# The feed-forward of the last block, computed in two groups of two windows

## The chip, the cores and the metric

The kernel runs on one core of a Trainium2 chip. A core has a matrix engine (TensorE, "PE" in the profile), a vector engine (VectorE, "DVE"), a scalar engine (ScalarE, "ACT"), GpSimd ("POOL") and SyncE ("SP"), which here issues all transfers. "PEld" is the loading of weights into the matrix engine, which the profile lists apart from the matmuls ("PE"). The metric is the device time of one execution in microseconds, as the median of several executions. All data are float32.

## The reference

The input is a batch of 2 sequences of 4096 tokens with 256 channels. First a residual recurrence (time mixing, a scan along the sequence, a group norm, an output projection), then a residual stack of two transformer layers. One layer is

```python
h = shift_token(x)                         # half of the channels from the token before
q, k, v = split(h @ wqkv, 3)               # 8 heads of 64
q, k = rotary_xpos(l2norm(q) * qs, l2norm(k) * ks)
x = x + local_attention(q, k, v) @ wo      # windows of 128, each looks at itself and the one before
h = layernorm(shift_token(x)) * lg + lb
a, g = split(h @ w1 + b1, 2)               # 256 -> 2 x 682
x = x + (a * gelu(g)) @ w2 + b2            # 682 -> 256
```

The last four lines are the feed-forward that the change touches. Every token's feed-forward needs only that token's `x` after attention and half of the channels of the token before.

## The kernel before, in words

Tokens are tiled into windows of 128 (`P`), four windows (`NW`) make a block of 512 tokens (`T`), and there are `NK` = 32 blocks (2 sequences, 2 layers, 8 blocks). The main loop of `tile_block_kernel` runs over `n`, one step for each of the `NN` = 128 windows. A step does the attention of window `n`, prepares the projections of window `n + 1`, and finishes window `n - 1`: `values` (probabilities times values), `output` (the projection by `wo`, added to `x`), `shift` (three or four small transfers that write the shifted copy of `x` into the tile `h`, and in the second layer an addition on GpSimd), and one step later `normed` (layer norm of that window in `h`).

The feed-forward goes by whole blocks of 512 tokens, spread over the steps of the blocks that follow. `transpose_h` (line 1244) transposes the four windows of `h` by TensorE into two banks of PSUM, and ScalarE and VectorE write them, scaled and shifted by the layer norm's weights, into `hT` (channels on the partitions, tokens along the row). `hidden` (1260) multiplies 128 of the 1364 hidden units (106 in the one remainder) by all 512 tokens: two matmuls, one for each half of the 256 channels. In the profile each float32 matmul is two records, so one call of `hidden` is four records of PE. `gate` (1268) copies such a bank into `hm`, five times; `remainders` (1271) does the last 42 gate units and the last 42 value units together and lays odd windows on other partitions than even ones, in `ends` and `rem`. `gelus` (1283) is one piece of seven activations on ScalarE that nothing may be put between. `value` (1294) multiplies five further banks into `hm` and `rem` into `ends`. `down_ends` (1313) begins the second product of two windows with the remainders, on half of the matrix rows each so that two matmuls run beside each other; `down` (1325) adds the five full parts, adds the result to `x` and stores the window to `out` (second layer).

`fill` (1338) says in which step each part is recorded: gates in the step with `s == 1` of the block after, the rest of the gates, the remainders, the gelus and two values in `s == 2`, the other values in `s == 3`, the two down products two blocks later. After the last window the loop runs on for six steps (`range(NN + 6)`, line 1447), in which no attention is left and only the feed-forward of the last block is recorded.

What is recorded is not the order on the engines. `Plan.note` (238) only records operations, with the row `plan.at` as their priority. `Plan.order` (376) then builds the order of all five engines with a list scheduler: it keeps a model of when each engine and each of the 8 banks of PSUM comes free, and on each engine always takes, among what could start first by the model, the piece with the lowest row. Matmuls into one bank that follow each other are one piece. `value` sets `plan.early` in the last block, which lets the value products be computed before the gelus that they are multiplied with. Semaphores are set by the tile framework for exactly the tiles and parts of tiles that overlap. Line 524, which most rows of the profile name, is the place in `Plan.give` from which every recorded operation is issued; the tiles' names tell the operations apart (`hT,w` into a bank: `hidden`; `w,hm`: `down`; `w,ends`: `down_ends`; `wo,oT`: `output`; `mats,h`: `transpose_h`).

Of the kernel before, what the change touches and what calls it, by code (L numbers as in the profile page):

```python
# [11 lines left out]
ALU = mybir.AluOpType  # L12
# [3 lines left out]
P = 128  # L16
# [5 lines left out]
NM = 6  # L22
HR = HID - 5 * P
HS = 64 + HR
HW = 10 * P + HS
T = 512
NW = T // P
# [153 lines left out]
class Plan:  # L181
# [35 lines left out]
    def bank(self, shape):  # L217

        return self.view(Place(T, True), 0, shape)
# [308 lines left out]
def kernel(ctx: ExitStack, tc: tile.TileContext, a: dict, out: bass.AP):  # L528
# [6 lines left out]
    tile_of, bank, piece = plan.tile, plan.bank, plan.piece  # L535
    act, dve, either = nc.scalar.copy, nc.vector.tensor_copy, nc.either.copy
# [4 lines left out]
    ident, gmat = (mats[:, i, :] for i in range(2))  # L541
# [318 lines left out]
    def weights(l, which):  # L860
        if "qkv" in which:
            for j in range(3):
                cols = slice(j * INNER, (j + 1) * INNER)
                nc.sync.dma_start(out=wqkv[:, :, cols], in_=a["w_qkv"][l][:, :, cols])
        if "o" in which:
            nc.sync.dma_start(out=wo, in_=a["w_o"][l])
        if "1" in which:
            nc.sync.dma_start(out=w1, in_=a["w_1"][l])
        if "2" in which:
            nc.sync.dma_start(out=w2, in_=a["w_2"][l])  # L870
# [370 lines left out]
            nc.gpsimd.tensor_tensor(x[:, w, :], x[:, w, :], x1s[k][:, w, :], ALU.add)  # L1241
            plan.at(row)

    def transpose_h(k):
        l = blocks[k][0]
        h = hs.pop(k)
        hT = hTs[k] = tile_of([P, 2, T], "hT")
        for i in range(2):
            pt = bank([P, T])
            for w in range(NW):  # L1250
                nc.tensor.transpose(
                    pt[:, w * P : (w + 1) * P], h[:, w, i * P : (i + 1) * P], ident
                )
            g, bb = lnp[:, l, 0, i : i + 1], lnp[:, l, 1, i : i + 1]
            if i == 0:
                nc.scalar.activation(hT[:, i, :], pt, AF.Identity, bias=bb, scale=g)
            else:
                nc.vector.tensor_scalar(hT[:, i, :], pt, g, bb, ALU.mult, ALU.add)

    def hidden(k, c0, cols):  # L1260
        pm = bank([P, T])
        for i in range(2):
            nc.tensor.matmul(
                pm[:cols], w1[:, i, c0 : c0 + cols], hTs[k][:, i, :], start=(i == 0), stop=(i == 1)
            )
        return pm

    def gate(k, m):
        either(hm[:, m, :], hidden(k, m * P, P))

    def remainders(k):
        pm = hidden(k, G_LAST * P, HS)
        rems[k] = tile_of([P, NW // 2, P], "rem")
        for odd in range(2):
            rows = slice(64 * odd, 64 * odd + HR)
            nc.scalar.copy(ends[rows], of_half(pm[64:HS], odd))
            either(rems[k][rows], of_half(pm[:HR], odd))

    def of_half(t, odd):

        return t.rearrange("p (w two t) -> p w two t", two=2, t=P)[:, :, odd, :]

    def gelus(k):
        l = blocks[k][0]
        with piece():
            for m in range(NM - 1):
                g = hm[:, m, :]
                nc.scalar.activation(g, g, AF.Gelu, bias=b1[:, l, 1, m : m + 1])
            for odd in range(2):
                rows = slice(64 * odd, 64 * odd + HR)  # L1290
                g = ends[rows]
                nc.scalar.activation(g, g, AF.Gelu, bias=b1[rows, l, 1, NM - 1 : NM])

    def value(k, m):
        l = blocks[k][0]
        plan.early = k == NK - 1
        if m < NM - 1:
            src = hidden(k, G_LAST * P + HS + m * P, P)
            g = hm[:, m, :]
            nc.vector.scalar_tensor_tensor(g, src, b1[:, l, 0, m : m + 1], g, ALU.add, ALU.mult)  # L1300
        else:
            src = rems.pop(k)
            for odd in range(2):
                rows = slice(64 * odd, 64 * odd + HR)
                g = ends[rows]
                nc.vector.scalar_tensor_tensor(
                    g, src[rows], b1[rows, l, 0, m : m + 1], g, ALU.add, ALU.mult
                )
        plan.early = False

# [2 lines left out]
    def down_ends(n):  # L1313

        k, i = (n - NW) // NW - 1, n % NW
        if not 0 <= k < NK or i > 1:
            return
        for odd in range(2):
            rows = slice(64 * odd, 64 * odd + 64)
            pys[k, 2 * i + odd] = bank([P, D])  # L1320
            nc.tensor.matmul(
                pys[k, 2 * i + odd], ends[rows, i, :], w2[rows, NM - 1, :], start=True, stop=False
            )

    def down(k, w):
        py = pys.pop((k, w))
        for m in range(NM - 1):
            nc.tensor.matmul(
                py, hm[:, m, w * P : (w + 1) * P], w2[:, m, :], start=False, stop=(m == NM - 2)
            )  # L1330
        x = xs[k][:, w, :]
        nc.vector.tensor_tensor(x, x, py, ALU.add)
        l, b, c = blocks[k]
        o = c * T + w * P
        to = out[b, o : o + P, :] if l else xmd[b][c][:, w, :]
        nc.sync.dma_start(out=to, in_=x)

    def fill(n, i):

        s = n % NW  # L1340
        k = n // NW - 2
        if s < 2 and 0 <= k < NK and i == 0:
            down(k, 2 * s)
            down(k, 2 * s + 1)
        k = n // NW - 1
        if not 0 <= k < NK:
            return
        if s == 1:
            gate(k, i)
        elif s == 2:  # L1350
            if i == 0:
                gate(k, 4)
                remainders(k)
                gelus(k)
            elif i < 3:
                value(k, i - 1)
        elif s == 3 and i < 3:
            value(k, i + 2)
            if i == 2:
                value(k, 5)  # L1360

# [80 lines left out]
    norms(0)  # L1444
    cosines(0)
    rotated(0)
    for n in range(NN + 6):
        k, w = divmod(n, NW)
        here, ahead, behind = n < NN, n + 1 < NN, 0 < n <= NN
        plan.at(n)  # L1450
        if here:
            transpose_qk(n)
        for c in range(rec2.n):
            if NW + 1 + int(c * R_SLOTS / rec2.n) == n:
                plan.at(n + 0.5)
                if AHEAD <= c + 1 < rec2.n:
                    rec2.ahead(c + 1, rec2.mixed)
                elif INSIDE <= c + 1 < AHEAD:
                    rec2.back(c + 1)
                rec2.scans(c)  # L1460
                if c + 1 == rec2.n:
                    rec2.group_norm()
        plan.at(n)

        first, l = ahead and (n + 1) % (NB * NW) == 0, ((n + 1) // (NB * NW)) % L
        if w == 3 and k + 2 < NK:
            load(k + 2)
        if w == 0 and k + 1 < NK:
            mixed_out(k + 1)
        if 1 < n < NN + 2:  # L1470
            normed(hs[(n - 2) // NW][:, (n - 2) % NW, :])
        if ahead:
            table(n + 1)
            if first:
                weights(l, "qkv")
            project(n + 1, 0)
            rotate(n + 1, 0)
        if here:
            scores(n)
            differences(n)  # L1480
        else:
            with piece():
                if n == NN:
                    values(n - 1)
                down_ends(n)
        if behind:
            kept(n - 1)
        if here:
            softmax(n, 0)
            softmax(n, 1)  # L1490
        if ahead:
            project(n + 1, 1)
            square(n + 1)
            rotate(n + 1, 1)
        if behind:
            output(n - 1)
            shift(n - 1)
            if here and n % (NB * NW) == 0:
                weights(n // (NB * NW) % L, "o")
        if w == 1 and 0 < k <= NK:  # L1500
            transpose_h(k - 1)
        if w == 2 and k + 1 < NK:
            transpose_x(k + 1)
        if here:
            softmax(n, 2)
            softmax(n, 3)
        if ahead:
            norms(n + 1)
        fill(n, 0)
        if here:  # L1510
            transpose_p(n, 0)
        if ahead:
            project(n + 1, 2)
            cosines(n + 1)
        fill(n, 1)
        if here:
            transpose_p(n, 1)
        if ahead:
            rotated(n + 1)
        fill(n, 2)  # L1520
        fill(n, 3)
        if w < 2 and NW < n < NN and (n - NW - w) % (NB * NW) == 0:
            weights(n // (NB * NW) % L, "12"[w])
    with tc.manual_schedule():
        plan.give()

# [78 lines left out]
```

## Time and profile before

| | before |
|---|---|
| median of three runs | 2972.16 us (2969.49 to 2972.76) |
| the profiled execution's own time | 2970.99 us |
| its span, first to last instruction | 2969.2 us |
| mean granted TensorE clock | 0.998 |
| PE busy, PE weight loads busy | 2945.0 us (99%), 1913.7 us (64%) |
| DVE, ACT, POOL busy | 2250.9, 2018.8, 1449.3 us |
| PE's instructions | 15548 |

Times in the profile are microseconds from the first instruction. A row of the timeline is a start, a length, an engine, a line, an operation, its output and inputs, the shape, and a count when equal instructions follow each other; a number in brackets is idle time before it and what ended that. [...] the start of the next row, not the end of the one before, tells how long a group held the engine.

### The profile page before, as it was taken

How to read it: one execution, taken by the hardware profiler on the slowest of the kernel's cores; microseconds unless marked ns; L12 is line 12 of the kernel's file. 1: busy time of each engine (PE TensorE's matmuls, PEld its weight loads, DVE VectorE, ACT ScalarE, POOL GpSimd, SP SyncE). 2: the span in 40 equal slices, each digit the busy share in tenths (PEclk: the TensorE clock that was granted, in tenths of full speed). 3: DMA queues.
4: the chain of work that ended last, by engine and by line, in shares of the span. 5: the costliest groups of instructions: out<-in, count | busy, mean ns of one | idle time of the engine just before them, and what ended most of it. 6: DMA issues, size and time to landing. Idle time of an engine off the chain costs nothing.

```text
span 2969.2 us, 48964 instructions
## 1 busy us (share of the span) xinstructions
PE 2945.0 (99%) x15548; PEld 1913.7 (64%) x15548; DVE 2250.9 (76%) x5088; ACT 2018.8 (68%) x5359; POOL 1449.3 (49%) x1705
## 2 busy tenths in 40 slices
PE   9999999999999999999999999999999999999998
PEld 4476766666666666666666666666666666666665
DVE  7889999998866788786777677777676676767673
ACT  7887787778666777776666666666666666666663
POOL 2226654555554555445555444545454554555550
PEclk9999999999999999999999999999999999999999
DMA  2324322221121211111122221111112211111110
GB/s 85 114 78 133 115 69 87 75 82 53 60 65 54 83 48 53 56 59 55 52 77 79 74 68 48 61 58 61 55 44 70 70 57 49 58 55 54 47 40 27
DMA packets 185227, 195.09 MB, mean 66 GB/s; under 512 B 27812, under 2 KB 148484, under 8 KB 184456
## 3 DMA queue, kind: packets, MB, share of 16 engines
q1 hardware_dynamic: 184968, 191.96, 20.9%
q8 instruction: 123, 2.02, 0.3%
q14 instruction: 136, 1.11, 0.1%
HBM read 85.46 MB, written 39.85 MB: 42 GB/s over the span
## 4 chain that ended last, share of the span: by engine, by line
PE 92%; DVE 3%; ACT 3%; issue 1%; POOL 0%; DMA 0%; SPq 0%; POOLq 0%; ACTq 0%; DVEq 0%
PE bank L524 92%; ACT pr L524 1%; ACT L524 1%; DVE arena L524 1%; DVE bank L524 0%; ACT pr L520 0%; DVE sq L524 0%; DVE qk L524 0%; DVE h L524 0%; DVE nmx L524 0%; DVE hm L524 0%; DVE pB L524 0%; ACT arena L524 0%; ACT oT L524 0%; ACT hm L524 0%
## 5 line engine op out<-in xcount | busy, mean ns | idle before, releaser
L524 PE MATMUL bank<-wqkv,xT 128*128 128x512 f32 x1536 | 723.8, 596 | 0.5 <-ACT xT L524 0.5
L524 PE MATMUL bank<-hT,w 128*128 128x512 f32 (+1 forms) x1408 | 652.2, 595 | 0.0
L524 POOL TENSOR_TENSOR t<-qk,tab 128x256 f32<-128x256 f32 x512 | 383.6, 768 | 471.2 <-ACT qk L524 362.3
L524 ACT ACTIVATE pr<-bank,nmx 128x129 f32<-128x129 f32 (+1 forms) x1024 | 369.5, 379 | 147.8 <-DVE nmx L524 146.4
L524 PEld LDWEIGHTS bank<-hT,w 128*128 128x128 f32 (+1 forms) x1408 | 254.8, 189 | 260.9 <-issue 247.3
L524 PEld LDWEIGHTS bank<-wqkv,xT 128*128 128x128 f32 x1536 | 266.4, 191 | 210.9 <-issue 207.3
L524 POOL TENSOR_TENSOR rn<-rn,mhalf 128x16 f32<-128x16 f32 x128 | 391.7, 3060 | 8.8
L520 ACT ACTIVATE pr<-pr,sums 128x129 f32<-128x129 f32 (+1 forms) x948 | 334.1, 418 | 40.7 <-DVE pr L524 39.9
L524 DVE COPY_PREDICATED bank<-packs,bank 128x254 f32<-128x254 int32 x496 | 186.4, 420 | 229.8 <-PE bank L524 229.7
L524 PE MATMUL bank<-w,hm 128*128 128x256 f32 x1280 | 294.0, 381 | 0.0
L524 POOL TENSOR_TENSOR dv<-vr,vt 128x512 f32<-128x512 f32 x124 | 165.4, 1334 | 201.2 <-PE bank L524 188.1
L524 PEld LDWEIGHTS bank<-w,hm 128*128 128x128 f32 x1280 | 239.7, 190 | 35.0 <-issue 4.2
L524 ACT COPY qk<-bank 128x512 f32<-128x512 f32 x225 | 132.3, 588 | 170.5 <-PE bank L524 164.0
L524 PE MATMUL bank<-kT,qT 64*128 64x256 f32 (+1 forms) x2048 | 246.1, 380 | 0.4 <-ACT kT L524 0.4
L524 PE MATMUL bank<-wo,oT 128*128 128x256 f32 x1024 | 243.0, 380 | 1.4 <-ACT oT L524 1.3
L524 PEld LDWEIGHTS bank<-wo,oT 128*128 128x128 f32 x1024 | 193.4, 190 | 70.5 <-ACT oT L524 22.6
L524 PEld LDWEIGHTS bank<-kT,qT 64*128 64x128 f32 x2048 | 190.4, 187 | 68.8 <-issue 36.0
L524 DVE TENSOR_TENSOR pB<-bank,backs 128x512 f32<-128x512 f32 x248 | 170.0, 686 | 83.5 <-PE bank L524 56.7
L524 ACT ACTIVATION_READ_ACCUMULATOR pr<-bank,nmx 128x1 f32 x1024 | 221.8, 217 | 0.0
L524 ACT COPY hm<-bank 128x512 f32<-128x512 f32 x170 | 99.8, 587 | 174.1 <-PE bank L524 173.1
L524 PEld LDWEIGHTS bank<-mats,pr 128*128 128x128 f32 x1148 | 134.9, 135 | 115.7 <-issue 73.2
L524 PE MATMUL bank<-pT,vt 128*64 128x128 f32 x2048 | 203.3, 279 | 0.0
(159 smaller groups left out, 5625.3 us busy)
## 6 DMA issues: line engine op xcount, KB each, us to landing
vr<-vt SPq DMA_DIRECT2D x124, 224.0 KB
tab<-in_c_rot_dram SPq DMA_DIRECT2D x128, 128.0 KB
kT<-kT SPq DMA_DIRECT2D x64, 256.0 KB
z<-zd SPq DMA_DIRECT2D x16, 512.0 KB
x<-in_x_dram SPq DMA_DIRECT2D x16, 512.0 KB
x1d<-x SPq DMA_DIRECT2D x16, 512.0 KB
x<-x1d SPq DMA_DIRECT2D x16, 512.0 KB
h<-x SPq DMA_DIRECT2D x128, 64.0 KB
```

Of the source, the lines that this page charges most:

```text
L520: self.nc.scalar.activation(dst, src, AF.Copy, scale=scale)
L524: getattr(getattr(self.nc, o.eng), name)(*args, **kw)
```

## The change

In the loop, the last block's feed-forward is no longer recorded: the loop ends after `NN + 2` steps, `fill` stops before block `NK - 1`, and the transposes of that block are left out. Instead `last_block` is called after the loop. It takes the block's windows 0 and 1, and then 2 and 3, and records for each pair the whole feed-forward: transposes, five gates, the remainders, the gelus, six values and the two down products, at row `NN` for the first pair and `NN + 2` for the second (the down products are recorded in the row set there, too). For that `transpose_h`, `hidden`, `gate`, `remainders`, `gelus` and `value` take a stretch of tokens `ts`. All other blocks are computed as before, with 512 tokens in one piece.

```diff
@@ -1241,15 +1241,17 @@
             nc.gpsimd.tensor_tensor(x[:, w, :], x[:, w, :], x1s[k][:, w, :], ALU.add)
             plan.at(row)
 
-    def transpose_h(k):
+    def transpose_h(k, w0=0, w1=NW):
         l = blocks[k][0]
-        h = hs.pop(k)
-        hT = hTs[k] = tile_of([P, 2, T], "hT")
+        h = hs[k]
+        if w0 == 0:
+            hTs[k] = tile_of([P, 2, T], "hT")
+        hT = hTs[k][:, :, w0 * P : w1 * P]
         for i in range(2):
-            pt = bank([P, T])
-            for w in range(NW):
+            pt = bank([P, (w1 - w0) * P])
+            for w in range(w0, w1):
                 nc.tensor.transpose(
-                    pt[:, w * P : (w + 1) * P], h[:, w, i * P : (i + 1) * P], ident
+                    pt[:, (w - w0) * P : (w - w0 + 1) * P], h[:, w, i * P : (i + 1) * P], ident
                 )
             g, bb = lnp[:, l, 0, i : i + 1], lnp[:, l, 1, i : i + 1]
             if i == 0:
@@ -1257,54 +1259,57 @@
             else:
                 nc.vector.tensor_scalar(hT[:, i, :], pt, g, bb, ALU.mult, ALU.add)
 
-    def hidden(k, c0, cols):
-        pm = bank([P, T])
+    def hidden(k, c0, cols, ts):
+        pm = bank([P, ts.stop - ts.start])
         for i in range(2):
             nc.tensor.matmul(
-                pm[:cols], w1[:, i, c0 : c0 + cols], hTs[k][:, i, :], start=(i == 0), stop=(i == 1)
+                pm[:cols], w1[:, i, c0 : c0 + cols], hTs[k][:, i, ts], start=(i == 0), stop=(i == 1)
             )
         return pm
 
-    def gate(k, m):
-        either(hm[:, m, :], hidden(k, m * P, P))
-
-    def remainders(k):
-        pm = hidden(k, G_LAST * P, HS)
-        rems[k] = tile_of([P, NW // 2, P], "rem")
-        for odd in range(2):
-            rows = slice(64 * odd, 64 * odd + HR)
-            nc.scalar.copy(ends[rows], of_half(pm[64:HS], odd))
-            either(rems[k][rows], of_half(pm[:HR], odd))
+    ALL = slice(0, T)
+
+    def gate(k, m, ts=ALL):
+        either(hm[:, m, ts], hidden(k, m * P, P, ts))
+
+    def halves(ts):
+
+        pairs = slice(ts.start // (2 * P), ts.stop // (2 * P))
+        return [(odd, slice(64 * odd, 64 * odd + HR), pairs) for odd in range(2)]
+
+    def remainders(k, ts=ALL):
+        pm = hidden(k, G_LAST * P, HS, ts)
+        if ts.start == 0:
+            rems[k] = tile_of([P, NW // 2, P], "rem")
+        for odd, rows, pairs in halves(ts):
+            nc.scalar.copy(ends[rows, pairs], of_half(pm[64:HS], odd))
+            either(rems[k][rows, pairs], of_half(pm[:HR], odd))
 
     def of_half(t, odd):
-
         return t.rearrange("p (w two t) -> p w two t", two=2, t=P)[:, :, odd, :]
 
-    def gelus(k):
+    def gelus(k, ts=ALL):
         l = blocks[k][0]
         with piece():
             for m in range(NM - 1):
-                g = hm[:, m, :]
+                g = hm[:, m, ts]
                 nc.scalar.activation(g, g, AF.Gelu, bias=b1[:, l, 1, m : m + 1])
-            for odd in range(2):
-                rows = slice(64 * odd, 64 * odd + HR)
-                g = ends[rows]
+            for odd, rows, pairs in halves(ts):
+                g = ends[rows, pairs]
                 nc.scalar.activation(g, g, AF.Gelu, bias=b1[rows, l, 1, NM - 1 : NM])
 
-    def value(k, m):
+    def value(k, m, ts=ALL):
         l = blocks[k][0]
         plan.early = k == NK - 1
         if m < NM - 1:
-            src = hidden(k, G_LAST * P + HS + m * P, P)
-            g = hm[:, m, :]
+            src = hidden(k, G_LAST * P + HS + m * P, P, ts)
+            g = hm[:, m, ts]
             nc.vector.scalar_tensor_tensor(g, src, b1[:, l, 0, m : m + 1], g, ALU.add, ALU.mult)
         else:
-            src = rems.pop(k)
-            for odd in range(2):
-                rows = slice(64 * odd, 64 * odd + HR)
-                g = ends[rows]
+            for odd, rows, pairs in halves(ts):
+                g = ends[rows, pairs]
                 nc.vector.scalar_tensor_tensor(
-                    g, src[rows], b1[rows, l, 0, m : m + 1], g, ALU.add, ALU.mult
+                    g, rems[k][rows, pairs], b1[rows, l, 0, m : m + 1], g, ALU.add, ALU.mult
                 )
         plan.early = False
 
@@ -1343,7 +1348,7 @@
             down(k, 2 * s)
             down(k, 2 * s + 1)
         k = n // NW - 1
-        if not 0 <= k < NK:
+        if not 0 <= k < NK - 1:
             return
         if s == 1:
             gate(k, i)
@@ -1358,6 +1363,23 @@
             value(k, i + 2)
             if i == 2:
                 value(k, 5)
+
+    def last_block():
+
+        k = NK - 1
+        for w in (0, 2):
+            plan.at(NN + w)
+            ts = slice(w * P, (w + 2) * P)
+            transpose_h(k, w, w + 2)
+            for m in range(NM - 1):
+                gate(k, m, ts)
+            remainders(k, ts)
+            gelus(k, ts)
+            for m in range(NM):
+                value(k, m, ts)
+            down_ends(NN + NW + w // 2)
+            down(k, w)
+            down(k, w + 1)
 
 
 
@@ -1444,7 +1466,7 @@
     norms(0)
     cosines(0)
     rotated(0)
-    for n in range(NN + 6):
+    for n in range(NN + 2):
         k, w = divmod(n, NW)
         here, ahead, behind = n < NN, n + 1 < NN, 0 < n <= NN
         plan.at(n)
@@ -1497,7 +1519,7 @@
             shift(n - 1)
             if here and n % (NB * NW) == 0:
                 weights(n // (NB * NW) % L, "o")
-        if w == 1 and 0 < k <= NK:
+        if w == 1 and 0 < k < NK:
             transpose_h(k - 1)
         if w == 2 and k + 1 < NK:
             transpose_x(k + 1)
@@ -1521,6 +1543,7 @@
         fill(n, 3)
         if w < 2 and NW < n < NN and (n - NW - w) % (NB * NW) == 0:
             weights(n // (NB * NW) % L, "12"[w])
+    last_block()
     with tc.manual_schedule():
         plan.give()
 
```

## The prediction

> **What bounds the kernel now.** I read the page first, then the timeline of the matrix engine (PE) in the last 55 us, then the chain of waits there, then the other engines' timelines.
>
> ```profile
> PE 2945.0 (99%) x15548; PEld 1913.7 (64%) x15548; DVE 2250.9 (76%) x5088; ACT 2018.8 (68%) x5359; POOL 1449.3 (49%) x1705
> PE 92%; DVE 3%; ACT 3%; issue 1%; POOL 0%; DMA 0%; SPq 0%; POOLq 0%; ACTq 0%; DVEq 0%
> ```
>
> PE is busy for 99% and is 92% of the chain: only PE's idle time, or its own work, can move the end. The built orders are the same on all engines up to the last transposes of probabilities, so the change concerns what stands from 2915 us on:
>
> ```profile
> 2914.56 0.89 PE L524 MATMUL bank<-mats,pr 128*128 128x128 f32 x5
> 2915.38 0.70 PE L524 MATMUL bank<-w,ends 64*128 64x256 f32 x4
> ...
> 2922.43 0.70 PE L524 MATMUL bank<-w,ends 64*128 64x256 f32 x4
> 2923.06 2.43 PE L524 MATMUL bank<-w,hm 128*128 128x256 f32 x10
> 2925.32 1.89 PE L524 MATMUL bank<-wo,oT 128*128 128x256 f32 x8
> 2927.05 2.32 PE L524 MATMUL bank<-w,hm 128*128 128x256 f32 x10
> 2929.21 0.49 PE L524 MATMUL bank<-mats,h 128*128 128x128 f32 x3
> 2934.43 1.33 PE L524 MATMUL bank<-mats,h 128*128 128x128 f32 x5 [4.74 <-DVE h L524]
> 2935.78 20.10 PE L524 MATMUL bank<-hT,w 128*128 128x512 f32 x44
> 2955.81 0.70 PE L524 MATMUL bank<-w,ends 64*128 64x256 f32 x4
> 2956.44 4.58 PE L524 MATMUL bank<-w,hm 128*128 128x256 f32 x20
> 2960.95 0.70 PE L524 MATMUL bank<-w,ends 64*128 64x256 f32 x4
> 2961.59 4.58 PE L524 MATMUL bank<-w,hm 128*128 128x256 f32 x20
> ```
>
> After three transposes PE has nothing left until 2934.43: the last window's `h` is not ready. The chain shows what it waits for, behind the down product that SP's queue puts ahead of the last transfer:
>
> ```profile
> 2929.41 0.43 DVE x L524
> ...
> 2930.25 1.96 DMA h<-x
> ...
> 2933.96 0.42 DVE h L524
> ```
>
> And PE comes back at a lower clock. The windows of the trace (after the stretch and its length: busy time and count of PE, PEld, DVE, ACT, POOL, then the granted clock):
>
> ```profile
> 2930.00:2940.00 10.00, 5.55 (x13) 2.93 (x14) 1.83 (x4) 1.36 (x2) 1.49 (x3) 0.83 0.05 16
> 2940.00:2950.00 10.00, 10.00 (x24) 4.33 (x24) 0.42 (x1) 4.49 (x8) 0.00 (x0) 1.00 0.00 0
> ```
>
> **What a half costs on PE.** A call of `hidden` is four records of 512 columns now, eight of 256 after: 88 instead of 44. In full flow ScalarE's copies of the gates start 1.72 us apart, so a 512-column record takes 0.430. A 256-column one on the full array is `wo,oT`: 2927.05 - 2925.32 = 1.73 for 8, 0.216. The 88 cost 19.01, the 44 cost 18.92: 0.1 us lost. What could make this wrong is the 44 added weight loads, 190 ns each (1024 loads for `wo,oT` in 193.4 us of the page). [...] The row speaks otherwise: load and matmul one after the other would be 0.40 us a record, and measured is 0.216 with all 128 rows. I go by the row.
>
> **The walk.** Order after, from the built program, priced by the rows above. At 2915.38 four transposes of windows 0 and 1 are put in (0.109 each, 8 of `mats,qk` in 0.87): 2915.81. Remainders of two down products 0.63, first down 2.26: 2918.70. The first value of the first pair, four records, moved up here: 0.86. Then attention's values, remainders, second down (2920.53 to 2925.32, with 0.09 for the change of array shape ahead, 4.88) and `wo` 1.73: 2926.2. It was 2927.05: one down product less now stands ahead of it. Third down 2.16: 2928.3. Its store still stands ahead of the last `h` transfer in SP's queue, so `h` is ready 2934.38 - 2929.21 = 5.2 later, at 2933.5. PE doesn't wait for it now: five gates, the remainder and four values of the first pair 10 x 0.864, 2937.0; last old down 2.16, 2939.1.
>
> Then the first pair's down products need its gelus, which only begin when all gates are copied. ScalarE's rows for this now:
>
> ```profile
> 2948.95 1.28 ACT L524 ACT_TABLE_LOAD   x1
> 2950.24 3.17 ACT L524 ACTIVATE hm<-hm,b 128x512 f32<-128x512 f32 x5
> 2953.32 1.02 ACT L524 ACTIVATE ends<-ends,b 42x256 f32<-42x256 f32 x2
> ```
>
> A copy of 512 takes 0.58 and of 256 takes 0.37, so 256 elements fewer save 0.21. A gelu goes from 0.62 to 0.41, one of `ends` from 0.51 to 0.40, a copy to `ends` or `rem` to 0.26. Counted from the first gate (2928.3): remainder readable at 6 x 0.864 + 0.2 = 5.4, four copies 6.4, table 7.7, five gelus 9.8, two more 10.6, VectorE's last multiplication (0.48 for 256, 0.37 for 128) 10.95 to 11.2. PE gets there at 8.64 + 2.16 + 0.09 = 10.9. Wait: 0.05 to 0.3, taken 0.15. The cover is the last old down product of 2.16; without it this wait would be 2.3. Remainders and two down products 2955.81 to 2960.95, 5.14: 2944.4.
>
> Only then come the second pair's transposes, by the built order. `h` is 11 us early. The second transpose starts 0.11 later and lasts 0.27, ScalarE begins `hT` at 0.42, 0.78 less 0.21, and PE at 1.04: 2945.5. Nothing covers these 0.6 us of waiting; before, the same wait was there at half clock. Eleven calls 9.50, 2955.0. The gelus of this pair need no table load: 6.4 + 2.05 + 0.8 = 9.3, but VectorE's order puts a value between the two `ends`, so the second is out at 9.65 to 10.1 and PE is there at 9.6: 0.1 to 0.6, taken 0.4. Change of shape 0.09, last remainders and down products 2960.95 to 2966.18, 5.23: PE ends at 2960.7 instead of 2966.2. **Sum: 5.5 us less.** As a balance: idle 4.9, transposes 1.35 and 0.33, half-clock gates 1.1 (2935.78 to the second gate's readable bank took 1.1 over full flow) go; 0.43 and 1.04 for transposes, 0.55 of waits, 0.1 of narrow matmuls come: 5.55.
>
> The remaining parts cost nothing that sets the end. ScalarE gets 18 instructions more and VectorE 7; what doesn't fall with the width is 0.37 - 0.21 = 0.16 for a copy, so some 3 and 1 us, and from 2920 to 2960 ScalarE was busy for 10.7 us and VectorE for 9.3. Banks: the gates of the first pair take those that additions to `x` leave, at the latest the third down product's (0.2 + 0.42 after 2928.3), for the remainder at 2932.6. SP gets no transfer more, and the last two stores stand as they stood, 3.0 us from PE's last matmul to the end of the span. POOL's last addition and norm come 0.9 earlier.
>
> **Row and rule on the clock.** In the profiled execution the stage at half clock cost some 1.6 us of the 5.5 (five transposes 0.5, gates 1.1). [...] By the row the change saves 5.5 in all[...]. The trace has one execution, so both ends stay; I take 5.3, nearer to the row, since it is the only one seen. The profiled time would go from 2970.99 to 2965.7, and the median, 1.2 higher, from 2972.16 to **2966.9**.
>
> **The rivals.** *The wait comes back as gelu waits* (0.08): ScalarE's gelus might cost 256 elements nearly what 512 do. Then each pair is 5 x 0.21 + 2 x 0.11 = 1.3 later, 2.5 in all, and 2969.4 results. For it: the piece is uninterrupted and both down products wait for its end; against: the copies' lengths fall with the width.
>
> *The weight loads set PE's pace* (0.08, the slower side). [...] Today there are 26 ns to spare (216 against 190). At 5.3/88 = 60 ns over 0.216 a record the gain is gone; with no overlap at all 88 x 0.19 = 16.7 is lost and the time is 2983.6. Against it: two thousand records of that width at 0.216. For it: none of them reads `hT` against `w1`.
>
> *The change doesn't fill the gap* (0.02), because the first pair waits for the whole of `h`: 2972. The waits in the built program name the parts of windows 0 and 1 alone, which are normed by 2905.74.
>
> **How the numbers follow.** The bound is 0.2%, 5.94 us, about what a measurement of this kernel can tell from no change. The walk as forecast has 0.82; its terms give 3.9 (clock) to 5.85 (no gelu wait), the runs shown scatter over 3.3 us, and a median after against a median before can well differ by 1.5 from it, so its own range is 2965.0 to 2969.0, and 0.45 of the 0.82 lie beyond the bound, 0.37 within. With the gelu waits 0.08 and the unfilled gap 0.02 within: same 0.47, slower 0.08. Range for 8 in 10: 2964.6 to 2969.6.
>
> **What would show it.** PE: no idle over 1 us between 2915 and the end, clock 1.00 throughout; `hT,w` rows of 256 with starts 0.216 apart; the second pair's first gate near 2945.5, the last matmul near 2960.7. ACT: one table load after 2915, gelus of 0.41. Wrong would be: a pace over 0.22, a wait over 1 us at either `w,ends`, or `h` later than 2944. A cold clock that timed runs don't have would show as a gain of the profiled span alone.

## The result, and the profile after

The median went from 2971.28 us (2969.31 to 2973.01, 18 runs) to 2965.59 us (2964.12 to 2966.97, 18 runs): 5.7 us less, ratio 0.9981 with a 95% interval of 0.9974 to 0.9988. The prediction was 2966.9. The gain, 0.19%, is on the line of 0.2% that the prediction drew, and its interval of 0.12 to 0.26% lies on both sides of it.

The profiled execution has a span of 2963.4 us, 5.8 less. Its timeline of PE from the last transposes of probabilities on (start, length, operation, tiles, shape, count; attention's values left out):

```profile
2913.89 0.90 PE L524 MATMUL bank<-mats,pr 128*128 128x128 f32 x5
2914.63 0.60 PE L524 MATMUL bank<-mats,h 128*128 128x128 f32 x4
2915.16 0.70 PE L524 MATMUL bank<-w,ends 64*128 64x256 f32 x4
...
2923.81 1.89 PE L524 MATMUL bank<-wo,oT 128*128 128x256 f32 x8
2925.53 2.32 PE L524 MATMUL bank<-w,hm 128*128 128x256 f32 x10
2927.69 8.80 PE L524 MATMUL bank<-hT,w 128*128 128x256 f32 x40
2936.32 2.32 PE L524 MATMUL bank<-w,hm 128*128 128x256 f32 x10
2938.58 0.94 PE L524 MATMUL bank<-w,ends 64*128 64x256 f32 x4
2939.45 4.58 PE L524 MATMUL bank<-w,hm 128*128 128x256 f32 x20
2943.87 0.60 PE L524 MATMUL bank<-mats,h 128*128 128x128 f32 x4
2944.91 9.76 PE L524 MATMUL bank<-hT,w 128*128 128x256 f32 x44 [0.44 <-ACT hT L524]
2954.60 1.22 PE L524 MATMUL bank<-w,ends 64*128 64x256 f32 x4
2955.75 4.58 PE L524 MATMUL bank<-w,hm 128*128 128x256 f32 x20
```

The 4.74 us of idle time are gone; 40 records of the first pair run, without a gap, between the third old down product and the last. The last matmul ends at 2960.33. Counted from the five transposes of probabilities, the last point before the two orders part, this stretch took 51.61 us before and takes 46.44. I call it the tail from here on. It is the better measure for small differences: what stands before it scatters from run to run by 2 us (those five transposes start anywhere from 2913.1 to 2915.2 in the twelve profiles of this study, with identical work ahead of them), and what follows it, PE's end to the span's, is 3.0 to 3.1 in each.

The windows of this profile show the clock at full speed all through, where it was 0.83 in one of them before (third number from the right):

```profile
2920.00:2930.00 10.00, 10.00 (x61) 8.52 (x58) 1.45 (x4) 1.33 (x3) 0.00 (x0) 1.00 0.12 39
2930.00:2940.00 10.00, 10.00 (x48) 8.23 (x47) 4.16 (x11) 6.23 (x15) 1.49 (x3) 1.00 0.01 3
2940.00:2950.00 10.00, 9.56 (x47) 8.15 (x46) 1.39 (x3) 2.42 (x6) 0.00 (x0) 1.00 0.12 39
```

### The profile page after: what moved, and what is told of

It reads as the page before. It is cut to its first block, busy times and chain, and to the rows that moved or that the text cites. A ratio compares the mean times of both kernels' runs of the same rounds, so it can differ in the third digit from the quotient of the medians.

```text
span 2963.4 us, 49081 instructions
## 1 busy us (share of the span) xinstructions
PE 2942.4 (99%) x15592; PEld 1919.1 (65%) x15592; DVE 2253.5 (76%) x5095; ACT 2023.8 (68%) x5377; POOL 1449.2 (49%) x1705
## 4 chain that ended last, share of the span: by engine, by line
PE 90%; DVE 5%; ACT 4%; issue 1%; DMA 0%; POOL 0%; ACTq 0%; DVEq 0%; POOLq 0%
PE bank L524 90%; ACT pr L524 1%; ACT L524 1%; DVE arena L524 1%; DVE sq L524 1%; DVE bank L524 1%; ACT pr L520 1%; DVE hm L524 0%; DVE nmx L524 0%; DVE qk L524 0%; DVE x L524 0%; DVE pB L524 0%; DVE rn L524 0%; ACT hm L524 0%; ACT arena L524 0%
## 5 line engine op out<-in xcount | busy, mean ns | idle before, releaser
L524 PE MATMUL bank<-hT,w 128*128 128x512 f32 (+2 forms) x1452 | 651.7, 582 | 0.4 <-ACT hT L524 0.4
L524 PEld LDWEIGHTS bank<-hT,w 128*128 128x128 f32 (+1 forms) x1452 | 262.7, 188 | 252.9 <-issue 237.7
L524 ACT COPY hm<-bank 128x512 f32<-128x512 f32 (+1 forms) x175 | 100.8, 576 | 178.3 <-PE bank L524 177.3
```

Source lines behind the costliest of these rows:

```text
L524: getattr(getattr(self.nc, o.eng), name)(*args, **kw)
```

## The experiments

The theory after the result: the gain is idle time that the first pair fills, and with it the half clock that followed the idle time (0.50 granted from 2934.4 to 2937 in the profile before); what is lost against that are three short waits. The rivals: going by pairs gains in itself; the narrow matmuls cost by their weight loads; the clock is a matter of chance and no part of the gain. Each time below stands against the kernel before as it was measured alongside that run, and each ratio is to that.

### Pairs without the filled gap

```diff
             ts = slice(w * P, (w + 2) * P)
-            transpose_h(k, w, w + 2)
+            if w == 0:
+                transpose_h(k)
             for m in range(NM - 1):
                 gate(k, m, ts)
```

> After, but the last block's transposes are made whole, for all four windows, so that no pair can begin before the last window is normed; gates, gelus, values and down products go by pairs as after. My theory: the whole gain is the idle time that the first pair fills, so it goes: idle 4.7 us and half clock as before, plus 0.1 for 88 narrow records instead of 44 and 0.5 for the last pair's wait for its gelus: 2971.3 + 0.6 = 2971.9. The rival that going by pairs gains in itself, gelus of one pair beside the other's gates: 2966 to 2969. The rival of the weight loads, 0.19 each in the open: 2980 or more.

Measured: 2972.17 us against 2971.5, ratio 1.0003 (0.9995 to 1.0011). The profile:

```profile
2929.85 0.49 PE L524 MATMUL bank<-mats,h 128*128 128x128 f32 x3
2935.07 1.33 PE L524 MATMUL bank<-mats,h 128*128 128x128 f32 x5 [4.73 <-DVE h L524]
2936.42 12.38 PE L524 MATMUL bank<-hT,w 128*128 128x256 f32 x52
...
2961.64 1.22 PE L524 MATMUL bank<-w,ends 64*128 64x256 f32 x4
2962.79 4.58 PE L524 MATMUL bank<-w,hm 128*128 128x256 f32 x20
```

The idle time is back and the whole gain is gone. Going by pairs gives nothing in itself. It costs the wait for the last gelus: 1.15 us from the start of the remainders' down products to the start of the full ones, where 0.63 would do. The first part of the theory stands.

### Idle time kept, clock kept up

```diff
         if w == 1 and 0 < k <= NK:
+            if k == NK:
+                pw = bank([P, D])
+                for _ in range(9):
+                    nc.tensor.matmul(pw, ident, xs[NK - 2][:, 1, :], start=True, stop=True)
             transpose_h(k - 1)
```

This is the kernel before with useless work in its gap.

> Before, with nine matmuls added that nobody reads: the last finished window of x against the identity, 256 columns, put between the last down product and the last transposes, so 3.9 us of useless work in the idle time of 4.7. The idle time stays lost; only the half clock is taken away. My theory, gain in two parts: the clock's part is what the half clock cost in the four profiles with the full idle time (five transposes 0.5 and gates 1.1 to 2.5, less the 0.2 that transposes at full clock must wait more for hT), so 1.4 to 2.9 less than before, about 2969.2. The rival that the clock costs nothing that sets the end: no change, 2971.2. The rival that useless work delays the transposes: longer by up to 0.5.

Measured: 2969.99 us against 2971.67, ratio 0.9994 (0.9986 to 1.0003). The interval holds 1 (2969.2 was expected), so the time alone doesn't settle it; the profile does:

```profile
2929.98 4.15 PE L524 MATMUL bank<-x,mats 128*128 128x256 f32 x18 [0.51 <-DVE x L524]
2933.97 1.33 PE L524 MATMUL bank<-mats,h 128*128 128x128 f32 x8
2935.74 19.15 PE L524 MATMUL bank<-hT,w 128*128 128x512 f32 x44 [0.43 <-ACT hT L524]
```

```profile
2935.00:2940.00 5.00, 4.57 (x13) 2.07 (x12) 0.81 (x1) 1.80 (x3) 0.00 (x0) 1.00 0.02 3
```

The 44 records of `hidden` take 19.1 us from first to next group, 0.43 each, from the first one on; before they took 20.0. The tail is 50.54. With the same idle time and no such work it was 51.61 in the profile before, 53.06 in its repeat and 52.27 in the first SP experiment below, which leaves the gap as it was. So the clock's part is 1.1 to 2.5 us and the rest, 50.54 - 46.44 = 4.1, is work moved into the gap, less the waits that the change brings.

### The kernel before once more

No edit.

> The kernel before, unchanged, run once more. Both theories of the time: ratio 1 within 0.1%. It is there for the clock after PE's idle 4.7 us ahead of the last transposes. If the half clock comes after every such idle time (what the one trace showed), the 10 us with the idle time have a granted clock near 0.83 again and the last five transposes take 1.3 us. [...]

Measured: 2971.06 us against 2971.5, ratio 0.9999 (0.9991 to 1.0007). The idle time is 4.74 again, and the half clock came and stayed longer (first the windows, then PE):

```profile
2930.00:2940.00 10.00, 5.25 (x13) 2.54 (x12) 2.24 (x5) 0.78 (x1) 1.49 (x3) 0.72 0.07 22
2940.00:2950.00 10.00, 10.00 (x23) 4.33 (x22) 0.24 (x1) 3.29 (x6) 0.00 (x0) 0.94 0.00 0
```

```profile
2935.01 1.33 PE L524 MATMUL bank<-mats,h 128*128 128x128 f32 x5 [4.74 <-DVE h L524]
2936.36 21.55 PE L524 MATMUL bank<-hT,w 128*128 128x512 f32 x44
```

Four profiles have this idle time, 4.73 to 4.79 us (before, this one, the one without a filled gap, the first SP experiment). In all four the transposes after it take 1.33 us, and the granted clock is low behind it: 0.50 from 2934.4 to 2937 in the profile before and from 2935 to 2940 in this one, 0.68 and 0.64 from 2935 to 2940 in the other two. The mean clock that is on record for every timed run, in three digits, says the same of the runs without a profile. Of 88 runs of kernels with this idle time (49 of before, 13 each of this one, the unfilled gap and the first SP experiment) none has 1.000. Of 20 runs of the 128-column kernel below, measured alongside and without the idle time, 8 have it. If a good part of the 88 had kept the clock up, some of them should have had it too. That I took 5.3 and not 5.5, to allow for executions that keep the clock up, was an estimate of mine; these runs show no such execution. What does change is how long it lasts: `hidden` took 21.47 us here from first record to the next group, 20.03 before.

### What ends the idle time

The prediction said that a down product's store stands ahead of the last transfer to `h` in SP's queue. Two runs on the kernel before moved a store behind that transfer, by a dependency that only the planner sees:

```diff
+        if n == NN - 1:
+            last_h.append(plan.pieces[-2][0])
...
+        for o in last_h if (k, w) == (NK - 2, 3) else ():
+            plan.hold = o
         nc.sync.dma_start(out=to, in_=x)
+        plan.hold = None
```

> Before, with one store moved: the last old down product's store stands behind the last transfer to h in SP's queue, not ahead of it; nothing else moves. My theory: the idle time ends when h is ready, and h is late by that store, so the transfer is issued at about 2928.96 instead of 2930.25, the idle time falls from 4.7 to 3.4 us and the time by 1.3, to 2970.0 (0.05%). [...] The rival that h is not what PE waits for: no change, idle time 4.7.

Measured: 2971.54 us against 2971.5, ratio 1.0001 (0.9993 to 1.0009), idle time 4.79 where 3.4 was expected. I had moved the wrong store: PE takes the four old down products in the order of windows 2, 3, 0, 1, so window 3's store was never the late one, and this run says nothing for or against the theory. SP's rows in this run still show a store, and then the transfer:

```profile
2929.44 0.34 SPq L524 DMA_DIRECT2D out_dram<-x  x1
2929.82 0.85 SPq L524 DMA_DIRECT2D h<-x  x1
```

The second run moves window 1's store instead (`(NK - 2, 1)` in the diff).

> Before, with the store that does stand between the transfers to h (that of window 1 of the block before, whose down product PE computes last) moved behind the last of them; nothing else moves. My theory: the last transfer is issued 1.3 us earlier, so PE's idle time falls from 4.7 to 3.4 us. If the half clock comes after such an idle time too, the time falls by 1.3, 2970.2; if it goes (or is shorter) by up to 2.9 more, since three repeats show its end anywhere from 3.5 to 6 us after the idle time: 2967 to 2970. The rival that h isn't what PE waits for: idle time 4.7, no change.

Measured: 2969.82 us against 2971.19, ratio 0.9995 (0.9987 to 1.0003), 1.4 us less by the medians, where 1.3 was expected if the half clock stays, with an interval that still holds 1. SP issues the three transfers in a row, and PE's idle time is what was forecast:

```profile
2926.29 2.11 SPq L524 DMA_DIRECT2D h<-x  x3
2928.51 0.48 SPq L524 DMA_DIRECT2D out_dram<-x  x1
```

```profile
2927.80 0.49 PE L524 MATMUL bank<-mats,h 128*128 128x128 f32 x3
2931.73 0.77 PE L524 MATMUL bank<-mats,h 128*128 128x128 f32 x5 [3.44 <-DVE h L524]
2932.93 20.85 PE L524 MATMUL bank<-hT,w 128*128 128x512 f32 x44 [0.43 <-ACT hT L524]
```

`h` is what PE waits for, and 1.3 us of it was the queue. The clock again fell: the five transposes ran faster than before (0.77 us instead of 1.33) and the gates after them slower than with the gap filled (20.78 us instead of 19.1); the granted clock was 0.82 from 2930 to 2935 and 0.84 from 2935 to 2940. The tail is 50.92.

### How near are 256 columns to the weight loads' pace

```diff
+        n = P if k == NK - 1 else T
+        for o in range(0, ts.stop - ts.start, n):
             for i in range(2):
                 nc.tensor.matmul(
-                    pm[:cols], w1[:, i, c0 : c0 + cols], hTs[k][:, i, ts], ...
+                    pm[:cols, o : o + n], w1[:, i, c0 : c0 + cols],
+                    hTs[k][:, i, ts.start + o : ts.start + o + n], ...
```

> After, but each product of w1 in the last block is made in matmuls of 128 columns instead of 256: 176 records instead of 88, same sums, same order. It asks how near 256 columns are to the pace of the weight loads (190 ns). My reading, loads beside matmuls and the longer of the two sets the pace: 0.19 a record instead of 0.108, 176 x 0.19 = 33.4 against 19.0, so 14.4 us more, 2980. [...] Loads without any cost: 2966.

Measured: 2966.49 us against 2971.5, ratio 0.9984 (0.9977 to 0.9991), 0.9 over the change's own median. My reading is off by far; loads without any cost, 2966, are what was measured. The groups of this run (busy time and mean length after the bar) say why:

```profile
L524 PE MATMUL bank<-hT,w 128*128 128x128 f32 x152 | 17.7, 276 | 0.4 <-ACT hT L524 0.4
L524 PEld LDWEIGHTS bank<-hT,w 128*128 128x128 f32 x152 | 17.4, 192 | 0.7 <-ACT hT L524 0.7
```

152 loads of 192 ns are 29.2 us of lengths in 17.4 us of busy time: loads overlap with each other as well as with matmuls. A record takes 17.7/152 = 0.116 us at most, against 0.216 for twice the columns. The tail is 47.49, 1.05 more than after. Without their waits the 176 records took 1.1 us more than the 88 did, and PE waits twice for ScalarE's copies of the remainders:

```profile
2932.72 4.04 PE L524 MATMUL bank<-hT,w 128*106 128x128 f32 x34 [0.35 <-ACT ends L524]
2950.68 4.93 PE L524 MATMUL bank<-hT,w 128*106 128x128 f32 x42 [0.35 <-ACT ends L524]
```

In turn PE comes late enough that both waits for gelus at the remainders' down products are gone (0.63 and 0.64 instead of 0.87 and 1.15), 0.76 less. So a load of 192 ns does not set the pace of these matmuls: there was no edge at 190 ns from which the change could have lost, and 128 columns cost 1.1 us here, not 14.

### The three waits that the change brings

First the second pair's transposes are put ahead of the first pair's down products, by recording them at a lower row:

```diff
-            transpose_h(k, w, w + 2)
+            if w == 0:
+                transpose_h(k, 0, 2)
...
+            if w == 0:
+                plan.at(NN - 0.5)
+                transpose_h(k, 2, 4)
+                plan.at(NN)
             down_ends(NN + NW + w // 2)
```

> After, with the second pair's transposes placed among the first pair's values instead of behind its down products; h is ready by then (2932.9 against about 2934.6). My theory: PE's wait for hT of 0.6 us (starts 2943.87 to 2944.91 for four transposes of 0.11) goes, nothing else changes, the last matmul ends 0.6 earlier: about 2965.0. The rival that transposes there delay the values and so the gelus' multiplications: the first wait at the remainders grows by 0.4 and the gain is 0.2.

Measured: 2964.31 us against 2971.19, ratio 0.9977 (0.9968 to 0.9986). The tail is 45.48, 0.96 less than after; 0.6 was expected:

```profile
2934.86 0.60 PE L524 MATMUL bank<-mats,h 128*128 128x128 f32 x4
2935.29 1.89 PE L524 MATMUL bank<-hT,w 128*128 128x256 f32 x8
2937.02 2.32 PE L524 MATMUL bank<-w,hm 128*128 128x256 f32 x10
2939.27 0.70 PE L524 MATMUL bank<-w,ends 64*128 64x256 f32 x4
2939.91 4.58 PE L524 MATMUL bank<-w,hm 128*128 128x256 f32 x20
2944.33 9.66 PE L524 MATMUL bank<-hT,w 128*128 128x256 f32 x44
2953.92 1.21 PE L524 MATMUL bank<-w,ends 64*128 64x256 f32 x4
```

The gates of the second pair follow the down products without a gap. And the first wait at the remainders is gone too: 0.63 from 2939.27 to 2939.91, where it was 0.87. The transposes, 0.43 long, now lie between the first pair's gates and its down products and so give the gelus time. I had counted them as neutral. With 0.1 less for the second pair's 44 records (9.59 us now, 9.69 after, where VectorE's half of `hT` was finished at 2945.05, 0.14 behind the start of the first record), the three sum to the gain: 0.6, 0.24 and 0.1.

Then the remainders' gelus first, in the last block alone (the diff shows the line in `last_block`; in `gelus` the two activations of `ends` are put ahead of the five of `hm` in the same way):

```diff
-            for m in range(NM):
+            for m in (NM - 1, *range(NM - 1)):
                 value(k, m, ts)
```

> After, with the two gelus of the remainders, and their multiplications, ahead of the other gelus of the pair instead of behind them (last block alone). My theory: the remainders' down products no longer wait at the second pair (0.52 us: 1.15 from the first to the full products instead of 0.63), so 0.5 less. At the first pair the built order now puts the remainders ahead of the last old down product, whose 2.16 us were the cover, so a wait of 0.3 to 0.5 stands there instead of 0.25. Net 0.3 less: 2965.3. If the waits are not the gelus' end, no change.

Measured: 2965.01 us against 2971.19, ratio 0.9979 (0.997 to 0.9987), tail 46.00: 0.44 less than after, 0.3 expected.

```profile
2935.66 1.02 PE L524 MATMUL bank<-w,ends 64*128 64x256 f32 x4
2936.61 6.74 PE L524 MATMUL bank<-w,hm 128*128 128x256 f32 x30
...
2953.92 0.70 PE L524 MATMUL bank<-w,ends 64*128 64x256 f32 x4
2954.55 4.58 PE L524 MATMUL bank<-w,hm 128*128 128x256 f32 x20
```

The second pair's wait is gone (0.63). The first pair's grew (0.95 from the remainders to the full products, 0.87 after), as feared, since the planner now takes the remainders ahead of the last old down product, which had covered them.

Both edits together:

> After, with both: the second pair's transposes early and the remainders' gelus first. My theory: the three waits of 0.6, 0.5 and 0.25 go, PE has no idle time from the last transposes of probabilities on, and PE's end is 1.2 to 1.35 earlier than after: 2964.3, ratio to before 0.9976. That is past 0.2%. If the waits only move to another place, 2965.0 to 2965.6.

Measured: 2964.16 us against 2971.19, ratio 0.9976 (0.9967 to 0.9985), tail 45.53, no better than the early transposes alone: the wait at the first pair (1.18 from remainders to full products) eats what the second gives. Here it is not the remainders' gelus that PE waits for: their last multiplication ends at 2936.29, before PE starts on them at 2936.46. The trace puts the wait in the middle of them down to VectorE's first multiplication into `hm`, which has just read a value product's bank:

```profile
2937.01 0.29 PEld L524 LDWEIGHTS bank<-w,ends 64*128 64x128 f32 x2 [0.26 <-DVE hm L524]
```

That PE waited for this bank to come free was not tried further.

Last, the early transposes with the remainders first only at the second pair:

> After, with the second pair's transposes early in both cases and the remainders' gelus first at the second pair alone, where no other work covers them; the first pair keeps the old order, with the last old down product as cover. My theory: no wait left on PE. From the start of the last five transposes of probabilities to the last matmul's end 45.48 (transposes early alone) less 0.52 = 44.96, against 46.44 after: 1.5 less than after, 2964.1 in time, ratio to before 0.9975. If the second pair's wait isn't the order of its gelus, 45.5 and 2964.6.

Measured: 2963.67 us against 2971.67, ratio to before 0.9975 (0.9965 to 0.9984), tail 44.98 where 44.96 was expected.

```profile
2937.17 2.32 PE L524 MATMUL bank<-w,hm 128*128 128x256 f32 x10
2939.42 0.70 PE L524 MATMUL bank<-w,ends 64*128 64x256 f32 x4
2940.05 4.58 PE L524 MATMUL bank<-w,hm 128*128 128x256 f32 x20
2944.47 9.66 PE L524 MATMUL bank<-hT,w 128*128 128x256 f32 x44
2954.07 0.70 PE L524 MATMUL bank<-w,ends 64*128 64x256 f32 x4
2954.70 4.58 PE L524 MATMUL bank<-w,hm 128*128 128x256 f32 x20
```

The profile lists no idle time of PE in the tail any more. This version has the lowest median of the study; against the change itself its interval overlaps, so that it is faster than that is shown by the tail (1.46 us), not by the times.

## Why the prediction was right

**The number.** 2966.9 was 1.3 us over the measured 2965.59. Of that, 0.9 is the starting point: the median of three runs before was 2972.16, that of 18 is 2971.28. The gain itself was taken as 5.3 and measured 5.7. That these two lie so close is in part luck, since errors of opposite sign stand behind them, as the next paragraphs show. On which side of the line of 0.2% the gain would fall the prediction had left open.

**The bound and the walk.** The steps can be laid beside the rows of after if 0.67 is added, the difference at the start of the tail. Start of the third old down product: 2926.2 forecast, 2925.53 + 0.67 = 2926.20. First gate 2928.3, and 2928.36. Ten calls of `hidden` 8.64, and 8.63. Transposes to the second pair's first gate 1.04, and 1.04. `h` was ready at 2932.92, 11 us before its transposes at 2943.87, as said. The tail should have been 2960.7 - 2914.56 = 46.1 and was 46.44.

**The terms that were mis-sized.** The wait for the first pair's gelus was taken as 0.15 and measured 0.24 (0.87 less 0.63), the second as 0.4 and measured 0.52; both lie in the ranges given. The eleven calls took 9.69 instead of 9.59 with the change of shape, 0.1 in the first record. Together 0.3. In turn the half clock cost more than the one trace before showed: that trace was at the short end of what its repeats show (tails of 51.61 against 52.27 and 53.06). That would account for the medians differing by 5.7 where the two first profiles' tails differ by 5.2. In that one trace itself the half clock cost less than the 1.6 of the prediction: 51.61 - 50.54 = 1.1 against the gap with useless work. The transposes' share was counted too high, 0.5: at full clock PE waits 0.43 for `hT` behind them, so from the first of the five to the first gate it took 1.20 in the second SP run and 1.35 in the trace before.

**The weight loads and the clock.** On weight loads the row was right: the ten calls before the last old down product took 8.63 us for 40 records, 0.216 each, beside loads of 190 ns, and the 16.7 us that no overlap at all would have cost did not come. The reason that I gave beside it, 26 ns to spare, was wrong: there is no such edge, as the 128-column run shows (0.116 us a record at most, with loads of 192 ns). On the clock I took 5.3, between the 5.5 of the row and the 3.9 of an execution that keeps the clock up; where between them was my estimate. The row was right again: the clock fell in all repeats (0.50, 0.68 and 0.64 granted from 2935 to 2940).

**The queue and the cover.** That SP's order makes `h` late was right and is shown by the second SP run, not by the first. That the last old down product covers the first pair's gelus fits the runs: with the cover moved away the wait grew from 0.24 to 0.32, although the gelus' order had been changed in its favour. The 2.3 that I gave as its price without cover wasn't tried with the old order of gelus.

**The other rivals.** ScalarE's gelus did fall with the width: five of 256 take 2.10 us, 0.40 from one to the next, with one table load in the tail. The gap was filled.

## What to carry to other kernels

Where one engine is busy for 99%, look for the one place where it isn't, and ask what is already ready there: splitting the last piece of a chain by its inputs' readiness moves work into the gap. The narrower matmuls cost next to nothing here at 256 columns (0.216 us a record, half of the 0.430 of 512) and 1.1 us in all at 128. Then price the small waits that the split multiplies (here the transposes' copy and the gelus' end, once per part) and give each another piece of work as cover; moving the cover away by a reordering gave part of the gain back. And when a queue is in order, a store that waits for late work holds up the transfer behind it: here moving one store was worth 1.3 us of idle time (4.74 to 3.44).

## What had not been expected of the hardware

Weight loads of 192 ns each, 152 of them in 17.4 us of busy time, followed one another at under 0.12 us, beside matmuls of 128 columns on the same rows. The granted clock fell behind each of the five idle times looked at. After 4.73 to 4.79 us it was 0.50 from 2934.4 to 2937 in the profile before, and 0.50, 0.68 and 0.64 from 2935 to 2940 in the three others; after 3.44 us it was 0.82 from 2930 to 2935 and 0.84 in the 5 us after that, with the five transposes still at 0.77 us. With the gap filled, where PE's longest idle time was 0.51, it was 1.00 from 2925 to 2945. How long it stayed low varied: the gates' group took 20.0 to 21.5 us, against 19.1 in the filled gap, so 1.0 to 2.4 more.
